# Layer 0 of a Perceiver kernel: a head bias and mask added by TensorE, table loads on another queue, and a drain written out by hand

## The chip, the cores and the metric

The kernel runs on one core of a Trainium2 chip. A core has a matrix engine (PE, with weight loads shown apart as PEld), a vector engine (DVE), a scalar engine (ACT), a general engine (POOL), and a sync engine (SP) whose queue issues most DMA transfers. Each engine works through its own list of instructions in order, and semaphores hold an instruction back until what it reads is there. The metric is device time in microseconds, lower is better.

## The reference, cut to what matters

A batch of 64 sequences with 32 tokens of 256 features goes through two layers of cross attention, self attention and a feed-forward network. The change lies in layer 0, whose two attentions and FFN input are:

```
x = x + xattn(ln(x), ctx)            # 16 heads of 16, causal: only the first 32 of 257 keys count
x = x + attn(ln(x))                  # 16 heads, gated, with a bias by distance:
    scores[n, s] = q[n] . k[s] / 4 + pos_bias[n - s, head]      for s <= n, else masked
    out = (softmax(scores) @ v) * sigmoid(x @ Wgate + bgate) @ Wout + bout
x = x + ffn(ln(x))                   # FFN input and weights are quantized and dequantized first:
    scale = max(|h|) / 32767;  h = round(h / scale) * scale     # one scale for the whole tensor
```

The FFN's single scale needs the greatest absolute value of the whole normalized input, so the first FFN product cannot begin before all of the gated attention is done.

## The kernel before, in words

**Tiling.** x stays on chip, 128 tokens (four sequences) a tile, 16 tiles. Layer 0 works on pairs of tiles, so there are eight pairs for the cross attention (`x` jobs) and eight for the gated self attention (`a` jobs). The 16 jobs are in the list `jobs`: x0 to x4, a0, x5, a1, x6, a2, x7, a3 to a7 (numbers 0 to 15).

**A pipeline written by hand.** The loop over t runs the jobs through five phases, one iteration apart: `proj` (job t), `soft` (t-1), `turn` (t-2), `sums` (t-3), `done` (t-4). Inside `tc.manual_schedule` every engine issues in the order in which the Python lines come; SP is not in that list. For a job:

- `stats_of_job` and `norm_job`: LayerNorm. DVE takes the statistics (L160, L161), POOL the inverse root (`rstd`, L163, L164), DVE normalizes (`xn`, L369), POOL adds the output bias row to x (L415).
- `inputs_job`: PE transposes xn (L381), ACT copies to `xT` (L385). `values_job` (PE L215, DVE `vz` L221), `queries_job` and `keys_products` (PE L397, ACT `qT` L410), `keys_apart` (ACT, eight instructions, `kb` L614), and for an a job `gate_job` (PE L397, ACT tanh L625).
- `scores_job`: PE multiplies queries with keys into PSUM `sc` (L265). For an x job PE first writes the causal mask into the same accumulation, as a product of the identity with `mask8` (L255). For an a job DVE adds the table `posb2`, bias plus mask, in `pair_masked` (L275). DVE takes the row maximum (L282) and in `shift_job` subtracts it (L287); ACT exponentiates (L704).
- turn: DVE sums (L291), takes the reciprocal, multiplies (L297) and transposes 32x32 blocks to `pt` (L302); ACT spreads pt over four sequences by masks to `pb` (`pair_spread`, L311, four instructions).
- sums: PE multiplies with the values (L323), and the result becomes `oT`, on ACT for an x job (L333), on DVE with the gate for an a job (L337); then `pair_out`: PE L348 and an add into x on DVE (L355, L357).
- done, for a jobs: `f0_input` in three steps, LayerNorm statistics, xn, and transposes to `f0_xT` with the running maximum `f0_mx` (L360).

Beside this, `dequantize` prepares the three FFN weights, a step per iteration (DVE L507 to L515, PE L523, ACT L526), and `lines_matrices` builds small constants for layer 1 in iteration 1. The loop runs to t=19; in the last four iterations nothing is projected and the pipeline drains. Then, in the pool `f0`, the greatest f0_mx is reduced over partitions on POOL (L882), the scale and its reciprocal are taken on DVE, f0_xT is rounded in eight DVE passes (L899, L900), and the first FFN products begin (L914). DVE also ors the bits of layer 1's FFN weights (`wck`) into `lost_bits` (L770), to see whether they can be handled at lower cost.

**Loads.** SP issues x, context and weights in the order of first use. ACT's queue issues cols, masks, two rows of biases, then the other seven rows (896 KB, one copy to each partition), `posb` (256 KB) and `x1_bvT`.

Of the kernel before, what the change touches and what calls it, by code (L numbers as in the profile page):

```python
# [66 lines left out]
def tile_perceiver(ctx: ExitStack, tc: tile.TileContext, d: dict, out: bass.AP):  # L67
# [39 lines left out]
    def load_rows(a, b):  # L107
        nc.scalar.dma_start(
            rows[:, a:b].rearrange("p r e -> p (r e)"), d["rows"][a * D : b * D].partition_broadcast(P)
        )  # L110

    load_rows(0, 2)
# [5 lines left out]
    nc.gpsimd.memset(mhalf, -0.5)  # L118

# [12 lines left out]
    posb2 = rowp.tile([P, 2, 2, 2, 4, L], F32, tag="posb2", name="posb2")  # L132

# [173 lines left out]
    def pair_spread(pool, pt):  # L307

        pb = pool.tile([P, 32, 4, L], F32, tag="pb", name="pb", bufs=2)
        for b in range(4):  # L310
            nc.scalar.activation(pb[:, :, b, :], pt, AF.Copy, scale=bmask[:, b : b + 1])  # L311
        return pb
# [108 lines left out]
    def lines_matrices(pool):  # L421
# [20 lines left out]
        nc.vector.tensor_scalar(js, jmat, col("plk")[:96], None, ALU.mult)  # L442
        pm = bank("mm")
# [7 lines left out]
        nc.vector.tensor_copy(own_head, pm[:, P : P + 8])  # L451
        pm = bank("mm")
# [74 lines left out]


    with (
# [24 lines left out]
        load_rows(2, NROW)  # L554
        posb = pool.tile([P, H, L], F32, tag="posb", name="posb")
        nc.scalar.dma_start(posb.rearrange("p h s -> p (h s)"), d["posb"])
        _r = _ROWS["x1_bv"] * D
        nc.scalar.dma_start(x1_bvT, d["rows"][_r : _r + D].rearrange("(m p) -> p m", p=P))
# [5 lines left out]
        dequantizing = dequantize(pool)  # L564
        mask8 = pool.tile([P, 8, L], F32, tag="mask8", name="mask8")

# [62 lines left out]
        def scores_job(w):  # L629

            if w["a"]:
                w["pe"] = pair_masked(pool, pair_scores(w["qT"], w["kb"]), posb2)
                w["mx"] = pair_max(w["pe"])
            else:
                sc = pair_scores(
                    w["qT"], w["kb"], mask=(ident, mask8.rearrange("p x s -> p (x s)"))
                )
                w["sc"] = sc.rearrange("p r (x s) -> p (r x) s", s=L)
                w["mx"] = pair_max(w["sc"])

        def shift_job(w):
            if w["a"]:
                pair_less(w["pe"], w["mx"])
            else:
                w["pe"] = pool.tile([P, 32, L], F32, tag="sm", name="sm", bufs=2)
                pair_less(w["sc"], w["mx"], w["pe"])
# [18 lines left out]
        with tc.manual_schedule(engines=hand_order):  # L665
# [4 lines left out]
            for t in range(NJ + 4):  # L670
                proj, soft, turn, sums, done = (job(t - k) for k in range(5))
                if t < 2:
                    values_job(proj)
                    keys_products(proj)
                if turn:
                    pair_times(turn["pe"], pair_rec(turn["pe"]))
                    turn["pt"] = pair_turn(pool, turn["pe"])
                if done and done["a"]:
                    f0_input(done, 0)
                if job(t + 1):  # L680
                    stats_of_job(job(t + 1))
                if sums:
                    sums["oT"] = pair_sums(pool, sums["pb"], sums["vz"], sums.get("gate"))
                if soft:
                    scores_job(soft)
                if proj:
                    inputs_job(proj)
                if done and done["a"]:
                    f0_input(done, 1)
                if proj and t >= 2:  # L690
                    values_job(proj)
                if soft:
                    shift_job(soft)
                if turn:
                    turn["pb"] = pair_spread(pool, turn["pt"])
                if done and done["a"]:
                    f0_input(done, 2)
                if sums:
                    if sums["a"]:
                        pair_out(sums["n"], sums["oT"], a0_wo, scale=0.5)  # L700
                    else:
                        pair_out(sums["n"], sums["oT"], x0_wo)
                if soft:
                    nc.scalar.activation(soft["pe"], soft["pe"], AF.Exp)  # L704
                if job(t + 1):
                    norm_job(job(t + 1))
                if proj:
                    queries_job(proj)
                    if t >= 2:
                        keys_products(proj)  # L710
                    keys_apart(proj)
                    gate_job(proj)
                if t == 0:
                    nc.vector.tensor_copy(mask8, bc(causal, 1, 8))
                elif t == 1:
                    lines_matrices(pool)
                    r2_a0 = row2(pool, "a0_bv")
                elif t == 2:


                    posr = posb.rearrange("p (m r h) s -> p m r h s", m=2, r=2)
                    for i2 in range(2):
                        for m in range(2):
                            for r in range(2):
                                nc.vector.tensor_tensor(
                                    posb2[:, r, i2, m], posr[:, m, r], bc(causal, 1, 4), ALU.add
                                )
                    posb2 = posb2.rearrange("p r i m h s -> p (r i m h) s")
                for _ in range(1 if t < NJ else 3):
                    next(dequantizing, None)  # L730
            for _ in dequantizing:
                pass

# [20 lines left out]
    lost_bits = rowp.tile([P, F1], I32, tag="posb2", name="lost_bits")  # L754
# [106 lines left out]
    magic = const.tile([P, 1], F32, tag="magic", name="magic")  # L861
    nc.gpsimd.memset(magic, MAGIC)
# [1066 lines left out]
```

## Time and profile before

| | us |
|---|---|
| three runs, median (lowest to highest) | 1338.08 (1337.02 to 1339.06) |
| the profiled execution | 1339.76 |
| its span, first to last instruction | 1338.0 |
| PE, DVE, ACT, POOL busy in the span | 1218.4, 919.9, 721.4, 165.5 |
| first product (L215) starts | 10.78 |
| sums of job 1 (L323 of t=4) start | 60.27 |
| sums of job 13 (L323 of t=16) start | 229.82 |
| first FFN product (L914) starts | 268.30 |

Times in a profile count from the start of the span. A row of a group gives line, engine, operation, output from input, shapes, count, busy time and mean duration in ns. A line of the waits gives who waited for whom: us in total, how often, and the longest. A piece of the chain gives start, duration, engine and line; "issue" is time in which the engine waited for nothing that the profile shows. "x8" after a matmul counts records, of which each fp32 matmul leaves two.

### The profile page before, as it was taken

Reading aid. Unit: us, or ns where it says so; the run is one execution under the profiler, and the core shown is the slowest. Engines: PE = TensorE matmul, PEld = TensorE weight load, DVE = VectorE, ACT = ScalarE, POOL = GpSimd, SP = SyncE. Lnnn points to the kernel's source line nnn. Section 1 sums busy time; section 2 is a strip of 40 time slices with the busy share of each in tenths; the row PEclk is TensorE's granted clock in tenths of the full one; section 3 lists DMA queues with packets and bytes.
Section 4 is the critical chain, followed back from the end, with each engine's and each line's share of the span. In section 5 each row is a group of like instructions: output and inputs, shape, how many; then the busy total and the mean of one; then the engine's idle time right before and its main releaser. Section 6 shows DMA issues by size and latency. Waiting matters only on the chain.

```text
span 1338.0 us, 27917 instructions
## 1 busy us (share of the span) xinstructions
PE 1218.4 (91%) x11438; PEld 945.1 (71%) x11438; DVE 919.9 (69%) x1793; ACT 721.4 (54%) x1515; POOL 165.5 (12%) x422
## 2 busy tenths in 40 slices
PE   5898998499969999999999999999768999999998
PEld 4687786344548777777777777777556888888887
DVE  3978889676994388779787888777767353353633
ACT  3688887326793356656666767666534321131311
POOL 3211211100001011221212121211100000000000
PEclk9999999899989999999999999999979999999999
DMA  9100020140132243111121111110016100000000
GB/s 244 19 9 26 2 80 14 48 157 0 32 113 69 89 124 92 38 53 46 52 57 46 53 45 46 37 29 2 2 29 197 62 16 1 16 1 0 17 0 18
DMA packets 63125, 66.28 MB, mean 50 GB/s; under 512 B 21072, under 2 KB 52624, under 8 KB 62992
## 3 DMA queue, kind: packets, MB, share of 16 engines
q1 hardware_dynamic: 61856, 62.75, 16.1%
q8 instruction: 92, 1.51, 0.5%
q10 hardware_dynamic: 1136, 1.68, 0.4%
q14 instruction: 41, 0.34, 0.1%
HBM read 57.53 MB, written 6.89 MB: 48 GB/s over the span
## 4 chain that ended last, share of the span: by engine, by line
PE 62%; DVE 23%; ACT 10%; issue 3%; DMA 2%; POOL 0%; SPq 0%; ACTq 0%; DVEq 0%; POOLq 0%
PE mm L1733 21%; PE mm L397 5%; PE mm L801 4%; PE mm L812 4%; PE pp L914 3%; PE mm L1222 3%; PE o L1060 3%; PE mm L215 2%; DVE mx L360 2%; DVE nm L1184 2%; PE o L1800 2%; PE o L348 2%; PE s L1173 2%; DVE pe L1203 2%; ACT kb L614 2%
## 5 line engine op out<-in xcount | busy, mean ns | idle before, releaser
L1733 PE MATMUL mm<-hl,f_h 128*128 128x512 f32 x1024 | 232.9, 389 | 1.2 <-ACT sl L1778 1.2
L1733 PEld LDWEIGHTS mm<-hl,f_h 128*128 128x128 f32 x1024 | 192.1, 188 | 41.3 <-issue 1.4
L801 PE MATMUL mm<-ct,x_wk 128*128 128x257 f32 x512 | 132.4, 402 | 14.8 <-ACT kb L807 13.5
L1191 ACT ACTIVATE pe<-s,nm 128x257 f32<-128x257 f32 x256 | 118.4, 483 | 45.5 <-DVE nm L1184 20.6
L1791 ACT ACTIVATE g<-mm,cols 128x512 f32<-128x512 f32 x64 | 44.1, 689 | 164.0 <-PE mm L1733 163.6
L1739 DVE CAST hl<-g 128x512 fp32r<-128x512 f32 x64 | 27.3, 426 | 147.7 <-ACT g L1791 147.7
L801 PEld LDWEIGHTS mm<-ct,x_wk 128*128 128x128 f32 x512 | 95.3, 196 | 37.1 <-ACT kb L807 15.5
L812 PE MATMUL mm<-x_wv,ct 128*128 128x256 f32 x512 | 121.1, 379 | 0.1
L812 PEld LDWEIGHTS mm<-x_wv,ct 128*128 128x128 f32 x512 | 97.0, 190 | 14.4 <-ACT vb L846 0.6
L1184 DVE TENSOR_REDUCE nm<-s 128x4 f32<-128x1028 f32 x64 | 78.1, 1221 | 14.8 <-PE s L1173 14.8
L807 ACT ACTIVATE kb<-mm,cols 128x257 f32<-128x257 f32 x128 | 57.8, 477 | 53.5 <-PE mm L801 49.7
L1211 POOL TENSOR_TENSOR px<-pe,rec 32x4 f32<-32x4 f32 x256 | 51.1, 200 | 274.8 <-DVE rec L1201 230.6
L1203 DVE TENSOR_SCALAR pe<-pe,rec 128x256 f32<-128x256 f32 x256 | 78.8, 370 | 5.4
L1222 PE MATMUL mm<-ident,pe 128*128 128x128 f32 x512 | 75.2, 281 | 7.1 <-DVE pe L1203 4.5
L1222 PEld LDWEIGHTS mm<-ident,pe 128*128 128x128 f32 x512 | 59.3, 141 | 23.5 <-issue 5.8
L311 ACT ACTIVATE pb<-pt,masks 128x1024 f32<-128x1024 f32 x64 | 68.3, 1142 | 6.3 <-DVE pt L302 5.7
L415 POOL TENSOR_TENSOR x<-x,rows 128x512 f32<-128x512 f32 x32 | 51.1, 1596 | 148.9 <-DVE xn L369 145.7
L1191 ACT ACTIVATION_READ_ACCUMULATOR pe<-s,nm 128x1 f32 x256 | 54.8, 214 | 0.0
L828 DVE COPY vb<-mm 128x512 f32<-128x512 f32 x55 | 37.7, 685 | 23.8 <-PE mm L812 21.2
L1227 DVE COPY pT<-mm 128x512 f32<-128x512 f32 x64 | 44.0, 687 | 11.2 <-PE mm L1222 9.4
L1173 PE MATMUL s<-kb,qb 32*64 32x257 f32 x1024 | 44.7, 400 | 7.4 <-ACT pe L1191 4.1
L914 PE MATMUL pp<-f_xT,wgtT 128*128 128x512 f32 x96 | 43.1, 612 | 7.3 <-DVE f_xT L900 7.3
(231 smaller groups left out, 2376.1 us busy)
## 6 DMA issues: line engine op xcount, KB each, us to landing
ct<-in_ctxT_dram SPq DMA_DIRECT2D x64, 257.0 KB, 2.8
raw<-in_f_h_dram SPq DMA_DIRECT2D x20, 512.0 KB, 4.3
wck<-in_f_h_dram SPq DMA_DIRECT2D x12, 512.0 KB, 4.0
raw<-in_f_w_dram SPq DMA_DIRECT2D x8, 512.0 KB, 3.8
dk<-kb SPq DMA_DIRECT2D x9, 257.0 KB, 3.2
kb<-dk SPq DMA_DIRECT2D x9, 257.0 KB, 2.7
dv<-vb SPq DMA_DIRECT2D x9, 256.0 KB, 3.1
vb<-dv SPq DMA_DIRECT2D x9, 256.0 KB, 2.7
```

The costliest lines, as they stand in the source:

```text
L311: nc.scalar.activation(pb[:, :, b, :], pt, AF.Copy, scale=bmask[:, b : b + 1])
L397: nc.tensor.matmul(pm[:, m * 2 * P : (m + 1) * 2 * P], lhsT=w[:, k, c0 + m * P : c0 + (m + 1) * P], rhs=src[:, k, :], start=(k == 0), stop ...
L801: nc.tensor.matmul(pm, lhsT=x1_wk[:, k, m * P : (m + 1) * P], rhs=ct[:, k, :], start=(k == 0), stop=(k == 1),)
L807: nc.scalar.activation(kb[:, m, :], pm, AF.Identity, bias=col("x1_bk", m))
L812: nc.tensor.matmul(pm[:, c * D : (c + 1) * D], lhsT=ct[:, k, c * P : (c + 1) * P], rhs=x1_wv[:, k, :], start=(k == 0), stop=(k == 1),)
L914: nc.tensor.matmul(pm[:, i, :], lhsT=w[:, k, m * P : (m + 1) * P], rhs=xT[:, 2 * n2 + i, k, :], start=(k == 0), stop=(k == 1),)
L1173: nc.tensor.matmul(sc[64 * m : 64 * m + 64, r, :S], lhsT=qb[rs, m, b % 4].rearrange("p h l -> p (h l)"), rhs=kb[rs, m, :], start=True, sto ...
L1184: nc.vector.tensor_reduce(w["nm"], w["sc"][:, :, :S], AX.X, ALU.max, negate=True)
L1191: nc.scalar.activation(w["pe"][:, r, :], w["sc"][:, r, :S], AF.Exp, bias=w["nm"][:, r : r + 1], accum_out=w["sums"][:, r : r + 1],)
L1203: nc.vector.tensor_scalar(pe[:, r, :SK], pe[:, r, :SK], rec[:, r : r + 1], None, ALU.mult)
L1222: nc.tensor.transpose(pt[:, r * P : (r + 1) * P], pe[:, r, c * P : (c + 1) * P], ident)
L1733: nc.tensor.matmul(pm, lhsT=w[:, k, c0 : c0 + P], rhs=hl[k][:, part, :], start=(k == 0 and part == 0), stop=(k == kt - 1 and part == 1),)
```

## The change

- `rows` 2 to 8, `posb` and `x1_bvT` are issued by SP, after x3 and before the weights of the gated attention.
- The bias and mask of the a jobs come as `bias8`, half the heads on each half of the partitions, and are added by PE through the identity, as the mask of x jobs is; `pair_masked` and posb2 are no longer used in layer 0, and lost_bits has memory of its own.
- `lines_matrices` is a generator, run in parts in iterations 5, 6, 7; `dequantize` runs two steps in iterations 1 to 3.
- A partition reduction of a constant is run on POOL at t=1.
- In the loop, f0_input's second step comes ahead of the scores; the out product comes after the transposes where an a job is projected, and last where an x job is.
- The loop ends at t=15, and the drain is written out; the spread of job 15 is shared by ACT and DVE.
- The FFN scale and the rounding move into the hand-written order; two of the eight passes go to ACT.

```diff
+    magic = const.tile([P, 1], F32, tag="magic", name="magic")
+    nc.gpsimd.memset(magic, MAGIC)
...
-    def pair_spread(pool, pt):
-        pb = pool.tile([P, 32, 4, L], F32, tag="pb", name="pb", bufs=2)
-        for b in range(4):
-            nc.scalar.activation(pb[:, :, b, :], pt, AF.Copy, scale=bmask[:, b : b + 1])
-        return pb
+    def by_column(on_dve, dst, src, scale):
+        if on_dve:
+            nc.vector.tensor_scalar(dst, src, scale, None, ALU.mult)
+        else:
+            nc.scalar.activation(dst, src, AF.Copy, scale=scale)
...
-        load_rows(2, NROW)
+        load_rows(nc.sync, 2, NROW)
         posb = pool.tile([P, H, L], F32, tag="posb", name="posb")
-        nc.scalar.dma_start(posb.rearrange("p h s -> p (h s)"), d["posb"])
+        nc.sync.dma_start(posb.rearrange("p h s -> p (h s)"), d["posb"])
...
+        def bias_heads():
+            posr = posb.rearrange("p (m r h) s -> p m r h s", m=2, r=2)
+            for r in range(2):
+                rs = slice(64 * r, 64 * r + 64)
+                for m in range(2):
+                    nc.vector.tensor_tensor(
+                        bias8[rs, m], posr[rs, m, r], bc(causal[rs], 1, 4), ALU.add
+                    )
...
         def scores_job(w):
+            add = bias8.rearrange("p m h s -> p (m h s)") if w["a"] else mask8.rearrange("p x s -> p (x s)")
+            sc = pair_scores(w["qT"], w["kb"], mask=(ident, add))
+            w["sc"] = sc.rearrange("p r (x s) -> p (r x) s", s=L)
+            w["mx"] = pair_max(w["sc"])
...
-            for t in range(NJ + 4):
+            for t in range(NJ):
...
                 if sums:
-                    sums["oT"] = pair_sums(pool, sums["pb"], sums["vz"], sums.get("gate"))
+                    sums_job(sums)
+                if f0:
+                    f0_input(done, 1)
                 if soft:
                     scores_job(soft)
-                if proj:
-                    inputs_job(proj)
-                if done and done["a"]:
-                    f0_input(done, 1)
-                if proj and t >= 2:
+                inputs_job(proj)
+                if sums and proj["a"]:
+                    out_job(sums)
+                if t >= 2:
                     values_job(proj)
...
+                keys_apart(proj)
+                gate_job(proj)
+                if sums and not proj["a"]:
+                    out_job(sums)
                 if t == 0:
                     nc.vector.tensor_copy(mask8, bc(causal, 1, 8))
                 elif t == 1:
-                    lines_matrices(pool)
                     r2_a0 = row2(pool, "a0_bv")
+                    warm = small.tile([P, 1], F32, tag="m2", name="warm")
+                    nc.gpsimd.partition_all_reduce(warm, eps, P, bass_isa.ReduceOp.max)
                 elif t == 2:
-                    posr = posb.rearrange("p (m r h) s -> p m r h s", m=2, r=2)
...
+                    bias_heads()
+                    lines_of = lines_matrices(pool)
+                elif t in (5, 6, 7):
+                    next(lines_of, None)
+                for _ in range(2 if 1 <= t <= 3 else 1):
                     next(dequantizing, None)
...
+            j12, j13, j14, j15 = jobs[NJ - 4 :]
+            weights_job(j14)
+            sums_job(j13)
+            scores_job(j15)
+            shift_job(j15)
+            spread_job(j14, 0, 2)
+            exp_job(j15)
+            spread_job(j14, 2, 4)
+            out_job(j13)
+            f0_input(j12, 0)
+            weights_job(j15)
+            f0_input(j12, 1)
+            spread_job(j15, 0, 4, dve=(1, 3))
+            sums_job(j14)
+            f0_input(j12, 2)
+            f0_input(j13, 0)
+            sums_job(j15)
+            f0_input(j13, 1)
+            out_job(j14)
+            f0_input(j13, 2)
+            f0_input(j14, 0)
+            out_job(j15)
+            f0_input(j15, 0)
+            f0_input(j14, 1)
+            f0_input(j15, 1)
+            f0_input(j14, 2)
+            f0_input(j15, 2)
+
+            sx, rx = scale_of(f0_mx, "x")
+            for st in range(NST):
+                xs = f0_xT[:, st].rearrange("p k n -> p (k n)")
+                if st % 2 == 0:
+                    nc.vector.tensor_scalar(xs, xs, rx, MAGIC, ALU.mult, ALU.add)
+                else:
+                    nc.scalar.activation(xs, xs, AF.Identity, bias=magic, scale=rx)
+                nc.vector.tensor_scalar(xs, xs, MAGIC, sx, ALU.subtract, ALU.mult)
...
-    lost_bits = rowp.tile([P, F1], I32, tag="posb2", name="lost_bits")
+    lost_bits = rowp.tile([P, F1], I32, tag="lost_bits", name="lost_bits")
```

## The prediction

> **What bounds the kernel now.** The stages first (busy time of each engine in four stretches: PE, PEld, DVE, ACT, POOL, granted clock, DMA share, GB/s):
>
> ```profile
> 0.00:60.00 60.00, 40.12 (x478) 31.51 (x478) 38.28 (x85) 29.42 (x49) 18.10 (x31) 0.94 0.60 142
> 60.00:230.00 170.00, 154.67 (x2242) 128.55 (x2244) 148.26 (x224) 138.72 (x228) 34.02 (x42) 0.99 0.08 26
> 230.00:268.00 38.00, 18.98 (x308) 14.82 (x300) 24.93 (x51) 15.89 (x23) 4.91 (x10) 0.82 0.14 49
> 268.00:311.00 43.00, 42.70 (x96) 18.94 (x97) 30.83 (x29) 11.14 (x11) 0.00 (x0) 0.96 0.38 123
> ```
>
> The change ends at 268, where the first FFN product (L914) starts; from there PE is full and the instruction order stays the same apart from DVE's first few. So the question is when L914 starts. Three stretches lead to it. In the head (0 to 60) the DMA share is 0.60. In the loop PE and DVE are both near 90%: neither alone bounds it. In the drain nothing is more than two thirds busy: it is latency. Next the waits. Head, then the loop (40 to 240):
>
> ```profile
> PE mm L215 <- DMA x_wv<-in_x_wv_dram: 10.8, 1, 10.8
> ...
> PE mm L381 <- DVE xn L369: 7.7, 3, 3.0
> PE sc L265 <- ACT kb L614: 7.1, 7, 1.4
> PE mm L215 <- ACT xT L385: 5.8, 8, 0.7
> PE o L323 <- ACT pb L311: 2.1, 1, 2.1
> ```
>
> PE's first product starts at 10.8, when x0_wv lands; in the loop PE loses about 20 us, always to a copy made just before. The DMA issues of the head show what x0_wv shares its engines with:
>
> ```profile
> rows<-in_rows_dram ACTq DMA_DIRECT2D x1, 896.0 KB, 8.6
> x_wv<-in_x_wv_dram SPq DMA_DIRECT2D x1, 256.0 KB, 8.9
> posb<-in_posb_dram ACTq DMA_DIRECT2D x1, 256.0 KB, 7.9
> ```
>
> Last the end of the drain, in the chain:
>
> ```profile
> 261.66 0.70 DVE f_mx L360
> 262.36 0.02 issue
> 262.39 0.17 DVE m L880
> 262.56 2.72 issue
> 265.28 0.39 POOL m L882
> ...
> 268.30 2.04 PE pp L914 x2
> ```
>
> The 2.72 us are POOL loading the code of its partition reduction: its configuration call stands at 259.6, right after its last LayerNorm step.
>
> **The change part by part.**
>
> *Tables behind the weights.* 896 + 256 KB leave the ACT queue and follow x3 on SP's. Before x0_wv lands some 1.15 MB less has to pass; at the 0.37 MB/us of that stretch this is 3.1 us, and ACT's and SP's streams no longer alternate: I take 3.7 (10.8 to about 7), between 1 and 4.5. Three issues of 0.4 us join SP ahead of a0_wqkv, which is needed only at t=5. posb is needed at t=2, rows 2 to 8 by POOL at the end of t=1 (about 26); 4.1 MB into the stream they land near 15. POOL's memset of lost_bits (0.96) now stands ahead of the first rstd, under the wait for x0_wv. The gain does not carry whole: the first FFN weight w, which t=1 now uses twice, lands after as many bytes as before (issued 19.8, 7.5 us), so near 26.8, an estimate from that row; DVE, 3.7 earlier than its xn at 29.1, is there at 25.4 and waits. lines_matrices has left t=1 (29.08 to 33.97 before, its PE waits included); the scale (2.4) and the first rounding (3.7) run: weights of t=2 start on DVE at 26.8 + 6.1 = 32.9 instead of 36.3.
>
> *The warm reduction at t=1.* POOL issues a code load, the reduction and a load back. Row: 5.65 us from POOL's previous end (259.63) to the reduction. For the way back:
>
> ```profile
> 529.53 0.38 POOL L1693 PARTITION_ALL_REDUCE lost<-lost  x1 [6.94 <-DVE lost L774]
> 537.01 0.95 POOL L1211 TENSOR_TENSOR px<-pe,rec 32x4 f32<-32x4 f32 x4 [7.10 <-DVE pe L1203]
> ```
>
> That product's reciprocal was ready at 530.5; it ran at 537.0, so going back costs up to 7.1. POOL is shut for 5.65 + 0.4 + 7.1 = 13.2 us from about 27, to 40.2. Queued behind is rstd of job 3 (1.6 with its slower first call: 41.8), and DVE's xn waits for it; DVE is there at 40.8. Cost 1.0; bounds 0 and 4 (POOL starting later). Against it: what does the warm run save at 262? The Trainium skill (GPSIMD Engine Reference, 2.1 Instruction dispatch) says that the first call of a freshly loaded kernel pays about 6 us more. The trace agrees for one load (5.65), and its 7.1 us way back, with code that had run just before, says that every switch is a fresh load. The changed program's POOL order keeps a load ahead of the real reduction. By row and rule the warm run saves nothing (0); if a second load were cheap, it saves the exposed 2.9. I take 0.
>
> *t=2 and t=3.* The posb2 table was eight DVE adds (8 x 0.28), now four (1.0); the second rounding (3.6) has gone to t=1, scaling (1.75) comes: t=3 starts on DVE at 45.3 instead of 50.0. On ACT, pt is ready at 36.9, then spread 4.3, exp 1.0, q 0.8, kb 3.7: t=3's scores get kb at 46.7 instead of 50.0. From there PE: the rest of the scores and the transposes 3.3, values, queries and keys 5.2, out 1.7, two groups of dequantizing transposes 0.9. Sums of t=4 start at 57.8 instead of 60.27: **2.5 us**, because the out product, which stood ahead of the keys, now ends the queue and the keys' copy runs beside it.
>
> *Bias and mask on PE.* Off DVE: L275, 1.22 x 8 = 9.8 us. On PE: 32 records per job. Price by starts in an x job:
>
> ```profile
> 156.56 0.66 PE L255 MATMUL sc<-mask,ident 64*32 64x256 f32 x16
> 157.02 0.42 PE L265 MATMUL sc<-kb,qT 64*32 64x128 f32 x16
> ```
>
> 0.46, and 0.43 for the second half: 0.9 x 8 = 7.2 us. It stands in front of the wait for kb, so up to 0.46 of each is free. sc is now held until the shift (L287), as x jobs hold it already.
>
> *The loop's new order.* I lay t=4 to 15 by hand with the chain's spacings. PE: sums 1.9, scores 2.1, transposes 0.6, each projection 1.73, FFN transposes 0.6, dequantizing group 0.44. DVE: weights 4.0, stats 1.05, max 1.2, shift 1.13, v add 0.6, x add 0.6, xn 0.65; oT 0.64 for an a job; FFN input 2.35; dequantizing 2.34, 3.6, 1.7; the lines 2.0 at t=5. ACT: spread 4.27, exp 1.05, q 0.8, kb 3.7, gate 0.8. In iterations that project an x job the out product now ends the queue and covers kb; in the others it covers xT; FFN xn moves ahead of the max. DVE's x add now stands last in x iterations, so DVE cannot begin the next weights before PE ends. Lengths on PE: 11.5, 14.2, 12.3, 16.6, 12.0, 14.6, 11.5, 15.5, 17.0, 14.3, 13.7, 14.3; sum 167.5. Of that about 159 is work. What is late next: at t=5 and 7 scores wait for kb (0.7, 2.1), as DVE carries the lines and dequantizing there; at t=11 FFN xn (1.6). At t=12 it is largest: DVE's x add of t=10 ends 0.6 after PE's last product of t=10, then come 2.3 of dequantizing, the 15.2 of t=11, and 5.7 of weights, stats and oT; PE needs that oT 18.7 + 1.6 + 0.6 after the same product, so out waits about 3, and values, which are queued behind it on PE, wait too. For seams I add 1.5: 169.0, where before took 229.82 - 60.27 = 169.55. So PE trades 20 us of waits for 7 of mask, some transposes pulled in from the drain, and 8 of new waits: **0.5 us**. f_up and f_dn loads move three iterations earlier on SP, past cT 7, whose buffer is not free earlier anyway.
>
> *Drain.* Before: 229.82 to 268.30, 38.5. By hand, from the last gate: sums of job 13, scores of 15, spread of 14 on ACT around one exp, weights of 15 done at +12.1, its spread half on DVE (2 x 0.74, by the row of the second layer's L1415) and half on ACT to +14.2, then oT, FFN stats, xn and max of jobs 13, 14, 15 mostly on DVE, the last rstd at +24.0, last max at +26.6. The code load starts only at +24.0: reduction +29.7 to +30.1 (3 us exposed), reciprocal +30.5. Rounding: DVE's order now has one or of lost_bits (1.22) between the two passes of the first quarter: first product 2.8 after the reciprocal, 2.25 before. 33.3 in all: **5.2 us**. ACT's two passes lie beside DVE's. The checking weights must have landed by then; they are issued behind oT in the drain as now (245.05), 4 us before landing.
>
> Sum: 2.5 + 0.5 + 5.2 = 8.2. The profiled execution took 1339.76 (span 1338.0 and 1.76 around it): 1331.6. It lies 1.7 above the median 1338.08, so 1329.9 on that scale: 1330.
>
> **The rivals.**
> *The warm run keeps the code at hand*: 2.9 less, 1327. For: the trace has no second load of this library whose end can be read; against: the 7.1 us way back.
> *The gains drown in the loop*: DVE's lag at t=5, 11 and 12 spreads and new waits are 14 instead of 8: 1336, within the noise. For: DVE and PE are within 4%; against: DVE has over 2 us less work than PE in six of the twelve (t=7, 8, 9, 13, 14, 15).
> *PE pays for the mask and keeps its waits* (slower): if kb, xT and xn still arrive late, the loop is 169.55 + 7.2 + the 7.5 of new stalls = 184, 15 above my layout: 1345. It decides once the loop is over 10 longer than before (7.7 of head and drain, and 2.7). For: DVE is chained to the end of PE's queue in x iterations; against: out gives 1.73 us of cover where the waits were 0.7 to 1.4.
> That the mask is not added on PE is excluded: the changed program's PE order has the same sixteen matmuls per a job that x jobs have.
>
> **How the numbers follow.** Forecast 0.53, warm run works 0.22, gains drown 0.14, PE keeps its waits 0.11. About 0.2% (2.7 us) can be told from no change. Faster: the first two and a little of the third, 0.78; same 0.12; slower 0.10. Low end: warm run works and the stalls at t=5 to 12 vanish, 1322; high end: drowned, 1338.
>
> **What would show it.** x0_wv's first product near 7; sums of t=4 near 57.8; L914 near 260, so L914 to the end unchanged (1070 us). POOL's reduction 5.6 us after its last rstd: reload; at once: rival one. PE's waits for kb, xT and xn in the loop at 8 us, not 20. Wrong if POOL's rstd at t=2 holds DVE for over 4 us, or if x0_wv still lands after 9.5.

## The result, and the profile after

The changed kernel takes 1336.3 us (median of 19 runs, 1330.63 to 1339.02) against 1339.06 us for the kernel before on the same chip (19 runs, 1333.38 to 1344.95): a ratio of 0.9969, with a 95% interval from 0.9954 to 0.9984 (the ratio is that of the means, 1335.4 and 1339.5; the medians lie closer together). By the interval that is a gain of 2.1 to 6.2 us. It is faster, by less than the 8.2 us of the forecast's sum. The profiled execution took 1338.12 us, its span 1336.3.

The three stretches ahead of the FFN, as in the table of stages before (busy time of PE, PEld, DVE, ACT, POOL, granted clock, DMA share, GB/s), for the kernel after:

```profile
0.00:60.00 60.00, 39.63 (x471) 31.45 (x472) 35.81 (x64) 29.12 (x48) 17.10 (x32) 0.89 0.59 142
60.00:230.00 170.00, 162.09 (x2521) 137.16 (x2523) 141.82 (x233) 139.98 (x235) 30.53 (x43) 0.99 0.09 28
230.00:268.00 38.00, 22.85 (x301) 15.83 (x294) 29.08 (x57) 13.78 (x18) 4.04 (x9) 0.78 0.21 70
```

In the loop PE has become busier by 7.4 us (154.67 to 162.09) and DVE less by 6.4: the mask has changed engines. From start to start its two products of a job hold PE for 0.46 and 0.43 us, 7.1 us over the eight jobs, which is the price that was worked out for it (7.2). What PE waits for in the head's end and the loop (40 to 240; us in total, times, longest):

```profile
PE mm L524 <- DVE w L516: 6.7, 1, 6.7
PE sc L265 <- ACT kb L650: 4.0, 7, 1.4
PE o L322 <- ACT pb L311: 3.8, 1, 3.8
PE o L347 <- DVE oT L336: 2.9, 1, 2.9
PE mm L380 <- DVE xn L368: 1.0, 1, 1.0
```

The waits for xT are gone and those for xn have shrunk from 7.7 to 1.0 us. But the first line is new, and it is one single wait. It leads back into the head. POOL at t=1 and t=2 (start, length, and in brackets the idle time ahead):

```profile
28.02 0.61 POOL L206 COPY row<-rows 128x512 f32<-128x512 f32 x1
34.40 0.57 POOL L767 PARTITION_ALL_REDUCE warm<-eps  x1 [5.76 <-issue]
42.51 0.18 POOL L163 TENSOR_TENSOR rstd<-mv,eps 128x2 f32<-128x2 f32 x1 [7.54 <-issue]
```

5.76 us of loading in front of the early reduction, 7.54 us of loading behind it, before POOL's next LayerNorm step, which nothing else held up: its releaser is "issue", and DVE had its input ready at 37.1. DVE stands behind it:

```profile
38.68 1.22 DVE L287 TENSOR_TENSOR sm<-sc,mx 128x1024 f32<-128x1024 f32 x1
43.55 0.74 DVE L368 TENSOR_SCALAR xn<-x,mv,rstd 128x256 f32<-128x256 f32 x2 [3.65 <-POOL rstd L164]
44.20 1.96 DVE L598 TENSOR_TENSOR bias<-posb,masks 64x128 f32<-64x128 f32 x4
46.17 1.76 DVE L516 TENSOR_TENSOR w<-w,s 128x1536 f32<-128x1536 f32 x1
```

and PE stands behind DVE:

```profile
48.08 1.09 PE L524 MATMUL mm<-ident,w 128*128 128x128 f32 x4 [6.69 <-DVE w L516]
49.09 2.83 PE L322 MATMUL o<-pb,vz 128*32 128x128 f32 x64
```

L524 is the transposing of the dequantized weights. A group of it closes t=2 in PE's queue and waits for the last of the DVE rows above. The sums of t=3 (L322) don't need those weights, but stand behind them, and start at 49.1 instead of 44.7. They also run longer, 2.83 us where before took 1.96. PE's granted clock from 46 to 52 (behind the busy times of the five engines) is 0.59, where before had 0.82:

```profile
46.00:52.00 6.00, 3.92 (x76) 3.30 (x84) 5.88 (x7) 0.58 (x1) 0.00 (x0) 0.59 0.00 0
```

The end of the drain, in the chain of waits:

```profile
256.48 0.17 DVE m L537
256.65 2.62 issue
259.27 0.39 POOL m L539
...
260.07 0.75 DVE f_xT L812
260.82 0.64 DVE lost_bits L853
...
261.87 0.76 DVE f_xT L815
...
262.76 37.46 PE pp L966 x83
```

After the last maximum on DVE 2.62 us of loading lie open in front of the reduction, where before had 2.72. L966 is the FFN product that was L914.

All profiled executions, by the start of PE's sums (L322, before: L323) at t=3, t=4 and t=16, of the first FFN product, and the time from there to the span's end; the last column is the ratio of the timed runs to those of before (the three repeats are single executions without one):

| kernel | t=3 | t=4 | t=16 | FFN | FFN to end | ratio, 95% interval |
|---|---|---|---|---|---|---|
| before, as shown | 44.7 | 60.3 | 229.8 | 268.3 | 1069.7 | 1 |
| before, second | 42.4 | 58.0 | 227.5 | 266.1 | 1069.2 | |
| before, third | 42.4 | 58.1 | 227.7 | 266.4 | 1071.0 | |
| after | 49.1 | 62.2 | 228.8 | 262.8 | 1073.5 | 0.9969 (0.9954 to 0.9984) |
| after, second | 47.4 | 61.8 | 226.8 | 260.8 | 1071.7 | |
| e1 no early reduction | 45.3 | 59.2 | 225.8 | 260.6 | 1073.6 | 0.9944 (0.9923 to 0.9966) |
| e2 dequantizing later | 40.4 | 58.9 | 226.1 | 261.6 | 1076.7 | 0.9946 (0.9929 to 0.9963) |
| e6 both | 41.2 | 55.7 | 222.2 | 255.9 | 1072.0 | 0.9923 (0.9901 to 0.9945) |
| e7 both, maximum by PE | 41.5 | 55.7 | 222.6 | 254.0 | 1074.7 | 0.9930 (0.9912 to 0.9949) |
| e9 both, tables back | 40.4 | 57.4 | 224.5 | 258.4 | 1076.5 | 0.9942 (0.9923 to 0.9961) |
| e11 both, and a delay | 41.1 | 55.9 | 224.2 | 267.9 | 1075.8 | 0.9997 (0.9982 to 1.0013) |
| e3 mask on DVE | 49.1 | 63.1 | 228.9 | 263.2 | 1073.8 | 0.9985 (0.9975 to 0.9995) |
| e8 order of before | 49.1 | 62.6 | 231.1 | 265.2 | 1074.5 | 0.9992 (0.9978 to 1.0006) |
| e4 tables only | 42.1 | 57.7 | 227.5 | 266.2 | 1074.0 | 0.9998 (0.9983 to 1.0013) |
| e5 drain only | 41.9 | 56.0 | 228.0 | 262.3 | 1078.9 | 0.9999 (0.9983 to 1.0015) |
| e12 drain only, again | 43.5 | 59.2 | 231.8 | 265.9 | 1073.0 | 0.9989 (0.9979 to 1.0000) |

The shown profile of before started the FFN some 2 us later than its two repeats, 266.2 on average. Against the repeats the two profiles of after (262.8 and 260.8) gain 4.5 us ahead of the FFN, which is what the ratio says (0.0031 of 1339 is 4.1).

### The profile page after: what moved, and what is told of

It reads as the page before. It is cut to its first block, busy times and chain, and to the rows that moved or that the text cites. A ratio compares the mean times of both kernels' runs of the same rounds, so it can differ in the third digit from the quotient of the medians.

```text
span 1336.3 us, 28421 instructions
## 1 busy us (share of the span) xinstructions
PE 1227.4 (92%) x11694; PEld 955.4 (72%) x11694; DVE 908.6 (68%) x1781; ACT 719.7 (54%) x1515; POOL 159.9 (12%) x423
## 4 chain that ended last, share of the span: by engine, by line
PE 64%; DVE 23%; ACT 7%; issue 3%; DMA 2%; POOL 1%; SPq 0%; DVEq 0%; ACTq 0%; POOLq 0%
PE mm L1779 21%; PE mm L396 5%; PE mm L884 5%; PE mm L895 4%; PE pp L966 3%; PE mm L1274 3%; PE o L1112 3%; PE mm L215 3%; DVE nm L1236 2%; DVE mx L359 2%; PE s L1225 2%; PE o L1846 2%; DVE pe L1255 2%; PE o L1294 2%; PE o L347 1%
## 5 line engine op out<-in xcount | busy, mean ns | idle before, releaser
L1779 PEld LDWEIGHTS mm<-hl,f_h 128*128 128x128 f32 x1024 | 192.2, 188 | 41.2 <-issue 1.4
L311 ACT ACTIVATE pb<-pt,masks 128x1024 f32<-128x1024 f32 x90 | 96.8, 1142 | 16.9 <-DVE pt L302 16.9
L890 ACT ACTIVATE kb<-mm,cols 128x257 f32<-128x257 f32 x128 | 57.7, 476 | 53.6 <-PE mm L884 49.8
L414 POOL TENSOR_TENSOR x<-x,rows 128x512 f32<-128x512 f32 x32 | 45.3, 1415 | 133.9 <-DVE xn L368 130.7
L384 ACT COPY xT<-mm 128x512 f32<-128x512 f32 x33 | 19.4, 587 | 61.9 <-PE mm L380 61.8
```

Of the source, the lines that this page charges most:

```text
L311: nc.scalar.activation(dst, src, AF.Copy, scale=scale)
L890: nc.scalar.activation(kb[:, m, :], pm, AF.Identity, bias=col("x1_bk", m))
L1779: nc.tensor.matmul(pm, lhsT=w[:, k, c0 : c0 + P], rhs=hl[k][:, part, :], start=(k == 0 and part == 0), stop=(k == kt - 1 and part == 1),)
```

## The experiments

**The head: early reduction, and PE's queue**

e1 takes the early reduction out of after.

```diff
                     r2_a0 = row2(pool, "a0_bv")
-                    warm = small.tile([P, 1], F32, tag="m2", name="warm")
-                    nc.gpsimd.partition_all_reduce(warm, eps, P, bass_isa.ReduceOp.max)
```

> After, without the early reduction on POOL at t=1. Theory (the head is lost to POOL changing its code back: 7.5 us before its reciprocal root of t=2, a wait of 3.65 us on DVE, and PE's queue behind it): the wait on POOL's rstd is gone from DVE at t=2, the sums of t=4 start 3 to 4.4 us earlier than in after (62.2), at 58 to 59, and the span falls by 3 to 4 us, to about 1332.5. The reduction of the drain still starts about 5.7 us after the last rstd, so the drain stays at 34. Rival (the early reduction loads the code for good, and the drain would be worse without it): the stretch from POOL's last rstd to its reduction grows by over 1 us. Second rival (the head is lost to PE's queue behind the dequantizing transposes alone, whatever POOL does): the sums of t=4 stay within 1 us of 62.

Measured: DVE's wait of 3.65 for POOL is gone (between 40 and 240 us it waits 0.5 for POOL's rstd in all), the sums of t=4 start at 59.2, 3.0 earlier than in after, the FFN 2.1 earlier. The reduction of the drain starts 5.62 us after POOL's last rstd, against 5.90 in after: the early one had not made it shorter. So the first rival falls, and the second one too, although PE's queue still loses something behind the same transposes:

```profile
44.33 1.09 PE L524 MATMUL mm<-ident,w 128*128 128x128 f32 x4 [4.53 <-DVE w L516]
45.35 3.62 PE L322 MATMUL o<-pb,vz 128*32 128x128 f32 x64
```

e2 keeps the early reduction and moves the first group of transposes from t=2 to t=3, so that they come behind the sums of t=3 in PE's queue: of six steps, two stay at t=1, one (DVE's scaling of the weights) at t=2, and three groups of transposes fall to t=3. e6 does e1 and e2 together.

```diff
-                for _ in range(2 if 1 <= t <= 3 else 1):
+                for _ in range({1: 2, 3: 3}.get(t, 1)):
```

> After, with its early reduction kept, and the dequantizing of the first group of weights put one round later (no step of it at t=2, so that its transposes stand on PE behind the sums of t=3). Theory (the 3.65 us on DVE cost the head only because PE's in-order queue stands behind the transposes that wait for DVE): the wait of 6.7 us of the transposes is gone at t=2, the sums of t=3 start about 45 to 46 rather than 49.1 (they wait for nothing that DVE's late chain makes), and the sums of t=4 come 2 to 4 us earlier, at 58 to 60; span about 1333 to 1334. Rival (DVE itself is the bound from t=2 on, so that the order on PE is indifferent): the sums of t=4 stay within 1 us of 62 and the wait shows at another instruction of PE (the scores of t=3 or t=4).

> After, without the early reduction and with the first group's dequantizing one round later, both at once. Theory: with POOL's code left as it is there is little left for PE's queue to wait for, so that this is within 1.5 us of the better of the two single changes (sums of t=4 at 57.5 to 59, span about 1332). Rival (two separate losses): the two gains add, sums of t=4 at 55 to 56.

In e2 POOL is as late as in after (its wait of 7.8 us is there, DVE's of 3.94 too), yet PE does not notice at t=3:

```profile
40.42 1.95 PE L322 MATMUL o<-pb,vz 128*32 128x128 f32 x64 [0.23 <-ACT pb L311]
```

40.4 was earlier than forecast (45 to 46): with nothing of DVE ahead of them the sums wait only for their own spread. The sums of t=4 come at 58.9, 3.2 earlier than in after. In e6 they come at 55.7, which is 6.5 earlier, about the two gains added (3.0 + 3.2), and 2.3 earlier than in the repeats of before; e7 and e11, whose head is that of e6, repeat it (55.7 and 55.9). So the rival of e6 was right, and the theory that there would be little left for the queue to wait for was wrong. e6's PE at t=3:

```profile
41.23 1.95 PE L322 MATMUL o<-pb,vz 128*32 128x128 f32 x64
...
45.57 0.45 PE L265 MATMUL sc<-kb,qT 64*32 64x128 f32 x16 [1.37 <-ACT kb L650]
```

The clock has a share in these gains that no run takes apart: from 46 to 52 us it was 0.77 in e1, 0.72 in e2 and 1.00 in e6.

e6's ratio of 0.9923 has an interval that does not meet that of after. e6 beats both kernels: 1330.0 us median of 6 runs against 1339.42 for before.

**The tables**

e4 is before with the three late loads on SP's queue and nothing else; e9 is e6 with them back on ACT's.

```diff
-        load_rows(2, NROW)
+        load_rows(nc.sync, 2, NROW)
...
-        nc.scalar.dma_start(posb.rearrange("p h s -> p (h s)"), d["posb"])
+        nc.sync.dma_start(posb.rearrange("p h s -> p (h s)"), d["posb"])
```

> Before, with the late tables put behind the first weights on SP's queue and nothing else changed. Theory (the tables' part of the change is sound and was only eaten in the head by the other parts): the first product starts at 8.3 as in after (before: 10.8), the weights of t=2 at 32 to 34 (before 36.3), the sums of t=4 at 58 (before 60.3), loop and drain as before (169.5 and 38.5); span about 1335.5 to 1336, a gain of about 2.3. Rival (the head is held by a later chain than the first weights, so the tables bring nothing): sums of t=4 within 0.6 of 60.3 and a ratio of 1.000. From the first FFN product to the end: 1069.7 if the 3.8 us that after lost there belong to the change, 1072 to 1075 if they belong to the execution.

e4's first product started at 8.06 and its FFN at 266.2, as the theory had it from the shown profile of before, but its ratio is 0.9998. The drain-only run, with its tables on the queue of before, gave the clue: its first product started at 8.15 as well. So before was profiled again.

> Before, unchanged, in another execution: what of the shown profile of before belongs to the kernel, and what to that one execution. The drain-only run had the tables on the queue of before, and its first product still started at 8.15 and not at 10.8. Theory (the 10.8 of the shown execution is chance, the tables cost the first weights nothing as a rule): first product at 8.0 to 8.3, sums of t=4 at 57.5 to 58, loop 169.5, drain 38.5, first FFN product at 265.7 to 266, and from there to the end 1072 to 1075, so that the whole is again about 1340. Rival (before is late at the first product in every execution): first product at 10.5 to 11, sums of t=4 at 60.3, from the first FFN product to the end 1069 to 1071.

> Before, unchanged, a third execution, to see the scatter of the stretch from the first FFN product to the end. Theory: first product at 8.0 to 8.3 as in most executions; the end stretch between 1070 and 1079, different from the second's by 1 to 4 us. Rival: first product at 10.5 to 11 and the end stretch within 1 us of 1069.7.

The first product of before (row of x0_wv's products), second execution:

```profile
L215 PE MATMUL mm<-x_wv,cT x32: 379/379/764, 8.1 to 52.5; 128*128 128x256 f32 x32
```

and of after, in the shown one:

```profile
L215 PE MATMUL mm<-x_wv,cT x32: 379/380/767, 8.3 to 55.8; 128*128 128x256 f32 x32
```

8.1 with the tables on ACT's queue, and 8.2 in the third execution. Over all the executions in the table: with the tables on SP's queue ten first products between 7.8 and 8.4; with them on ACT's six, of which four lie between 8.1 and 8.4, one at 9.4 (e12) and one at 10.8 (the shown one of before). So the wait that the first step of the forecast wanted to shorten is not there as a rule. It comes now and then, only with the tables on ACT's queue in this sample; the means are 8.8 and 8.2, so some 0.6 us may be had on average.

> After without the early reduction, with the first group's dequantizing one round later, and with the late tables put back on ACT's queue as in before. Theory (the queue of the tables is indifferent to the head): first product at 8.0 to 8.3, sums of t=4 at 55.7 and first FFN product at 255.9, each within 0.5 us of the run with the tables on SP's queue, and a ratio of about 0.992. Rival (the tables on ACT's queue delay the first weights): first product at 10.5 to 11, everything to the first FFN product 2.5 us later, ratio about 0.994.

e9's first product came at 8.4. Its sums of t=4 are 1.7 later than in e6 and its FFN 2.5 later, but not by the rival's mechanism: at t=3 ACT's kb is only 0.16 later. The rest is PE's clock, from 46 to 52 us 0.72 in e9 and 1.00 in e6:

```profile
46.00:52.00 6.00, 6.00 (x82) 4.88 (x63) 5.35 (x9) 3.14 (x5) 0.90 (x2) 0.72 0.00 0
46.00:52.00 6.00, 6.00 (x78) 5.19 (x59) 5.90 (x10) 4.38 (x5) 0.90 (x2) 1.00 0.01 3
```

PE is busy throughout in both, and 28% of 6 us is 1.7. The ratios, 0.9942 and 0.9923, overlap. By e4's interval a gain of up to 2.3 us is left open, by the first products some 0.6.

**The loop: mask or order**

e3 adds the bias and mask of the eight gated jobs on DVE again, in the order of after (the table for it takes DVE eight adds at t=2 instead of four). e8 keeps the mask on PE and puts the steps of a round in the order of before.

```diff
+            if w["a"]:
+                w["pe"] = pair_masked(
+                    pool, pair_scores(w["qT"], w["kb"]), posb2.rearrange("p r i m h s -> p (r i m h) s")
+                )
+                w["mx"] = pair_max(w["pe"])
+                return
```

> After, but the bias and mask of the eight gated jobs are added by DVE again, as in before (PE adds the mask of the cross jobs only, as before did in neither: those of the cross jobs stay as after has them). Theory (the loop gained 2.9 us because DVE was relieved): the loop from the sums of t=4 to those of t=16, 166.6 in after, grows by 2 to 4 us, and the drain is longer by up to 1. Rival (PE is the bound of the loop, and the mask's eight products of about 0.9 us each cost it 7 us there): the loop becomes 3 us or more shorter than 166.6.

> After, with the steps of a round in the order of before (out projection after the spreads, the FFN input's second step after the job's inputs), everything else as after. Theory (the mask on PE brought nothing in the loop, as the run with it on DVE shows: 165.8 from the sums of t=4 to those of t=16; the loop's 2.9 us come from the order of the out projection): the loop is 168.5 to 170 in place of 166.6, drain 34. Rival (neither alone, the two only together, or the dequantizing moved out of the loop): the loop stays within 1 us of 166.6.

From the sums of t=4 to those of t=16: before 169.6 (all three), after 166.6 and 165.0, e3 165.8, e8 168.5. Neither theory nor rival of e3 held: the loop is as long with the mask on DVE. What PE saves in e3 it waits. Its waits from 40 to 240:

```profile
PE sc L265 <- ACT kb L650: 8.1, 8, 1.7
...
PE o L322 <- ACT pb L311: 5.1, 1, 5.1
PE o L347 <- DVE oT L336: 3.3, 1, 3.3
```

and in e8:

```profile
PE mm L215 <- ACT xT L384: 5.8, 8, 0.7
PE sc L265 <- ACT kb L650: 4.7, 5, 1.2
```

The old order brings the eight waits for xT back, exactly 5.8 us as in before. The waits for xn (7.7 in before) stay away, and that goes with the mask: e12, in the same order with the mask on DVE, keeps 4.8 of them. So of the loop's gain 1.9 to 3.5 us would belong to the out product's new places, which cover ACT's copy of xT, and the mask by itself would be worth 0.8 us or less in the new order. Both sizes are uncertain, as e3 and e8 were profiled once: the eight executions with the loop of after (after, its repeat, e1, e2, e6, e7, e9, e11) scatter from 165.0 to 168.2. Over the whole run after stands at 0.9969 and e3 at 0.9985, with intervals that overlap.

**The drain**

e5 is before with the written drain, its shared spreads and the shared rounding. As the loop now ends at t=15 and dequantizing still goes one step a round, its last three groups of transposes also move: before ran them behind the sums of t=16, e5 runs them ahead of these.

```diff
-            for t in range(NJ + 4):
+            for t in range(NJ):
...
+            weights_job(j14)
+            sums_job(j13)
+            scores_job(j15)
```

> Before, with the written drain, its shared spreads and the shared rounding of the FFN's input, the tables on the queue of before and the loop in the order of before. Theory (the drain's 4.5 us are the written order's own, whatever comes ahead): sums of t=4 at 60.3 and of t=16 at 229.8 as in before, first FFN product 34 us after the latter (before 38.5); the first FFN product at about 263.8; span 1333.5 to 1335. Rival (the drain is shorter only because the loop ahead left less work open, or because the mask is on PE): the drain stays above 36.5.

From the sums of t=16 to the first FFN product: 38.5 to 38.7 in before's three executions, 34.3 in e5, 34.0 in both of after, 34.1 in e8. So the rival of e5 falls. But the sums of t=16 came 172.0 after those of t=4 (before 169.6), and the total did not move: part of the gain was only moved. In before:

```profile
229.82 1.96 PE L323 MATMUL o<-pb,vz 128*32 128x128 f32 x64
...
238.36 1.47 PE L523 MATMUL mm<-ident,w 128*128 128x128 f32 x12
```

and in e5:

```profile
225.07 1.04 PE L524 MATMUL mm<-ident,w 128*128 128x128 f32 x8
227.41 0.66 PE L524 MATMUL mm<-ident,w 128*128 128x128 f32 x4 [1.30 <-ACT kb L650]
228.00 1.95 PE L322 MATMUL o<-pb,vz 128*32 128x128 f32 x64
```

Ahead of the sums of t=16 the three groups and a wait take 2.9 us (in e12, the same program once more, 2.9 as well). It is the fault of t=2 in small: fillers ahead of urgent work. In after the double steps of t=1 to 3 have brought two of the three groups into earlier rounds, and only one, 0.5 us, stands there. From the sums of t=4 to the FFN, which counts the transposes on both sides, before takes 208.0 to 208.3, e5 206.3 and e12 206.7. So the written drain with these transposes in front of it is worth 1.3 to 2.0 us.

e7 is e6 with the FFN's first maximum over the partitions taken by PE.

```diff
-            sx, rx = scale_of(f0_mx, "x")
+            pm = bank("mm")
+            nc.tensor.transpose(pm[:1, :P], m1, ident)
+            m3 = small.tile([1, 1], F32, tag="m3", name="m3")
+            nc.vector.tensor_reduce(m3, pm[:1, :P], AX.X, ALU.max)
+            pm = bank("mm")
+            nc.tensor.matmul(pm[:, :1], lhsT=ones, rhs=m3, start=True, stop=True)
```

> After without the early reduction and with the first group's dequantizing one round later, and the FFN's first maximum over the partitions taken by PE and DVE (a transpose, a maximum over the row, a product with a row of ones) in place of POOL's reduction. Theory (the 5.9 us before POOL's reduction are its code coming in, of which some 2.5 lie after the partial maximum on DVE): from the partial maximum to the scale 1.5 us in place of 2.9, first FFN product 1 to 1.5 us earlier than without it (255.9), that is at 254.5 to 255; span about 1327. Rival (the second reduction of the FFN, which then is the first to need the code, waits longer by what was saved): the first FFN product comes earlier, but the way from it to the end grows by 1 us or more.

From the partial maximum to the scale's start e7's chain takes 1.73 us (250.22 to 251.95), where e6 took 2.88 (249.91 to 252.79):

```profile
250.22 0.17 DVE m L809
...
250.53 0.39 PE mm L811
...
250.94 0.29 DVE m L813
...
251.36 0.57 PE mm L815 x2
...
251.95 0.17 DVE s L817
```

The FFN starts at 254.0, 1.9 earlier than in e6 (lost_bits no longer falls between the rounding passes either). The way to the end is longer, but not as the rival said: POOL's next reduction had its code long since and waited for DVE's maximum alone:

```profile
300.83 0.38 POOL L539 PARTITION_ALL_REDUCE m<-m  x1 [53.72 <-DVE m L537]
```

The ratio (0.9930) is that of e6 within the interval.

**Behind the FFN's start**

The same instructions took 1069 to 1079 us there. Is this scatter, or does a gain made earlier get lost? The second execution of after, and two more timed runs:

> After, unchanged, in another execution. Theory: up to the first FFN product it agrees with the shown execution within 0.5 us (first product 8.3, sums of t=4 at 62.2, first FFN product at 262.8); from there to the end it scatters, 1070 to 1077. Rival (the 1073.5 us belong to the kernel): within 1 us of 1073.5 again.

a2 took 1071.7 us behind the FFN's start, 1.8 less than the first execution; and 2.0 less ahead of it. So single executions of one kernel differ by 2 us on either side (e5 and e12, below, by 3.6 ahead and 5.9 behind), and single profiles can't be compared more finely. The repeats of before took 1069.2 and 1071.0, where 1072 to 1075 was expected of the second execution.

That leaves a rival: all three executions of before took less than all thirteen of the other kernels (1071.7 to 1078.9). The granted clock speaks against a loss that the change makes there. Over the whole execution it was 0.976 to 0.978 in the three of before and 0.965 to 0.974 in the others. Among them is e4, which does there just what before does, and took 1074.0. Within one kernel time goes with it too: of after's 19 timed runs the fastest (1330.63) had 0.979, the slowest (1339.02) 0.969. And mostly the timed runs keep the gain of the FFN's start: against the repeats of before 4.5 us at the start and 4.1 by the ratio in after, 10.4 and 10.3 in e6, 7.9 and 7.8 in e9. The widest miss is e5 with 3.9 and 0.1. Whether the change itself lowers the clock a little is not shown.

> After without the early reduction and with the first group's dequantizing one round later, plus seven multiplications by one of the FFN input's first quarter on DVE between the scale and its rounding (7 of 0.75 us by the row of the first rounding pass, in order on DVE): pure delay, nothing else moves. Theory (what is gained or lost ahead of the first FFN product is carried to the end one to one, and the differences behind it are scatter of single executions): first FFN product 5.3 us later, at 261.2, and the total 5.3 us longer than without the delay, ratio 0.9923 + 0.0040 = 0.996, within 0.002. Rival (part of a gain ahead of the FFN is given back behind it, whatever the kernel): the total grows by less than 3 us, ratio under 0.9945.

```diff
             sx, rx = scale_of(f0_mx, "x")
+            for _ in range(7):
+                xs = f0_xT[:, 0].rearrange("p k n -> p (k n)")
+                nc.vector.tensor_scalar(xs, xs, 1.0, None, ALU.mult)
```

The delay came out larger than written: DVE's ORs of lost_bits fell in between, and one of them waited for its weights to land:

```profile
258.61 1.14 DVE lost_bits L854
259.76 0.02 issue
259.77 4.51 DMA wck<-in_f_h_dram
...
264.38 1.23 DVE lost_bits L854
```

From the sums of t=16 the FFN came after 43.8 us, not 33.7: 10.1 more than in e6. The ratio is 0.9997, which is 0.0074 or 9.9 us more than e6, with some 3.6 either way by the two intervals. So a shift of the FFN's start reaches the end, one to one within that; the forecast size was wrong, and the rival of e11 (less than 3 us) falls.

> The drain-only run once more, since its first product of the FFN came 3.9 us earlier than in the repeats of before and its total did not. Theory (scatter of that series): ratio 0.9965 to 0.9985, and from the first FFN product to the end 1070 to 1075. Rival (this kernel gives its gain back behind the FFN's start every time): ratio 0.9990 to 1.0010 again, and that stretch at 1077 or more with a granted clock near 0.67 between 940 and 1000.

The same drain-only kernel: 1073.0 us behind the FFN's start, and a ratio of 0.9989, between what theory and rival named. Counted from the first FFN product, e5 is 0.4 us behind e12 up to 929 us of its span and 5.8 from 1056 on: the two differ in the second layer's drain. The granted clock there in e5:

```profile
940.00:1000.00 60.00, 44.47 (x541) 33.50 (x540) 36.52 (x88) 23.57 (x42) 3.58 (x8) 0.67 0.01 2
```

and in e12, the same program:

```profile
940.00:1000.00 60.00, 41.61 (x576) 31.94 (x565) 40.72 (x97) 26.35 (x51) 4.36 (x12) 0.86 0.02 3
```

The clock (behind the five engines' busy times) is 0.67 and 0.86, with PE busy for 44.5 us instead of 41.6 (the same times in the two spans lie some 3 us apart in the kernel). The Trainium skill (TensorE: Matmul & The Clock Gate, part 1, "What's actually happening") says that the window over which PE's activity is judged runs freely and does not start with the kernel; two executions of one program with different clocks in a stretch full of gaps agree with that, but no run here shows the window itself. By their ratios e5 and e12 gain 0.1 and 1.5 us, with intervals that reach from 2 us lost to 2.8 gained. The 1.3 to 2.0 us from the sums of t=4 to the FFN, transposes counted, lie within both; the 4.5 us of the drain's own stretch do not.

## Why the prediction was right or wrong, point by point

- **Tables: wrong, in its premise.** 10.8 us for the first product was one execution's. The repeats of before stand at 8.1 and 8.2, after at 8.3; the step's 3.7 us (bounds 1 to 4.5) are 0 as a rule, and e4's ratio is 0.9998. A duration from one execution was taken as given, and the bound should have included zero. (The rate of 0.37 MB/us was high for that stretch, too: from 1.7 to 10.7 us the queues moved 304 GB/s, 0.30 MB/us.)
- **Early reduction: the right mechanism, the wrong size.** That every switch of POOL's code is paid was right: 5.76 us in and 7.54 back (forecast 5.65 and 7.1), and nothing saved at the end (reduction 5.90 us after the last rstd; between 5.6 and 6.2 in every execution with it, with or without the early run). POOL began to load at 28.6, not 27, and was back at 42.5, not 40.2, and DVE was ready at 39.9 instead of 40.8; so the wait was 3.65, not 1.0, inside the bound of 4. The rival that the early run works falls.
- **t=2 and t=3: the step that failed.** The layout counted the two groups of dequantizing transposes at the end of t=3 and left out the one at the end of t=2, so it had the sums of t=3 free and put the early reduction's cost at 1.0. That one group stands on PE ahead of everything of t=3, which is queued behind its wait for DVE (6.7 us). It asked who waits for POOL (DVE), not who waits for that (PE, through an instruction that is not urgent at all). The sums of t=4 came at 62.2 and 61.8 where 57.8 was said: 4.2 us. e1 and e2 each give back about 3, e6 with both 6.5. Against the repeats of before (58.0) the head lost 4.0 instead of gaining 2.5; without the two faults, in e6, it gains 2.3. The layout also took PE at full speed, where its clock was 0.59 just behind the wait.
- **Mask on PE: right in price, and in worth as far as shown.** 7.1 us on PE, against 7.2. With the mask back on DVE (e3) the loop is no longer than in after; a gain or loss inside the scatter of 3 us can't be seen.
- **Loop: 169.0 forecast, 166.6 and 165.0 measured.** The waits were forecast at 8 us and are 7.9 apart from the transposes' and one for pb (kb 4.0, oT 2.9, xn 1.0). The 1.5 us for seams and part of the laid-out lengths were too much: the longest of the eight executions with this loop is 168.2. The rival that PE keeps its waits falls: those for xT are gone, by the order and not by the mask, as e8 shows.
- **Drain: right.** 34.0 against 33.3, with the load exposed (2.6 us against 3) and the one lost_bits between the passes, as laid out. 4.5 to 4.6 us gained against 5.2. Up to 1.5 of them are the transposes that left the drain (PE's 1.47 us at 238.4 in before), which the layout had named; no run has the written order without this move.
- **Behind the FFN: right within the scatter, though the shown pair denies it.** 1073.5 against 1069.7 looks like a loss of 3.8. e11 shows a shift carried through, the repeats lie at 1069 to 1072, and the executions of before had the higher clock.

The sum is then -4.0 in the head, +3.8 in the loop (169.6 to 165.8, the mean of two) and +4.6 in the drain: 4.4 us, where 8.2 was forecast. The head alone is 6.5 off, the loop made up for 3.3 of it. The time lies where the rival of drowned gains was placed (1336), but not for its reason: the gains were not eaten by DVE's lag in the loop.

## What to carry to other kernels

When a change makes one engine late, follow the wait two engines down: the instruction that waits may be unimportant, and still hold a whole queue (here 6.7 us behind four transposes that nobody needed yet). Place such fillers behind the urgent work of the next round, not ahead of it. A code load that is run early to "warm" POOL was worth nothing here, as POOL did other work in between. A change of the schedule can also carry fillers from one side of a mark to the other: measure a stretch that holds them on both sides before a gain is put down to one of its parts. And before a forecast rests on the start of a single DMA, or a verdict on 2 us between two profiles, look at a second execution of the same kernel.

## What the runs showed of the hardware

- POOL's way back from the partition reduction costs as much as the way in, or more: 7.1 to 8.0 us in the five executions with the early reduction (7.54 in the shown one of after), against 5.6 to 6.2 for the way in. The loading starts at the end of POOL's last other instruction, not when the data is ready: e7, which left 53.72 us between, had no load to wait for.
- The landing of the first weights scattered with the same program: 6.3, 6.3 and 8.9 us from issue in before's three executions, 6.3 and 7.5 in the two of the drain-only kernel, 6.5 in e9, all with the late tables on ACT's queue; 6.0 to 6.6 in the ten with them on SP's.
- The granted clock in the same stretch of the same program (940 to 1000 us) was 0.67 in one execution and 0.86 in another, and the first took 5.4 us longer from 929 to 1056. At 46 to 52 us it was 0.72 in e9 and 1.00 in e6 with PE busy throughout in both; what set it is not shown.
